# Second-layer biases of a mixture of experts: one spread load per expert and one addition per block, or one gathered row per token

## The chip, the cores and the metric

The kernel runs on one core of a Trainium2 chip. The metric is the device time of one execution in microseconds (us), a median over runs. The profile is one further execution, recorded by the hardware profiler. TensorE (PE) does matmuls, VectorE (DVE) and ScalarE (ACT) work on tiles, GpSimd (POOL) issues transfers whose rows are picked by an index, and SyncE (SP) issues the large loads. Each engine works through its own list of instructions in the order in which it was built.

## The reference, cut to what matters

625 tokens of width 768 pass a two-layer graph attention network, and then a transformer block whose second half is a mixture of 8 experts with one expert per token. With one expert per token the weight of the choice is a softmax over one value, so it is 1.

```python
x = x + _L0_gnn_ref(_layernorm(x), edge_index, ...)          # two graph attention layers
x = x + _L0_ffn_ref(_layernorm(x)[None], ...)[0]
# inside _L0_ffn_ref:
x = x + out @ Wp + bp                                         # after causal attention, 12 heads
h2 = _ln(x, ln2_g, ln2_b).reshape(-1, d)
w, sel = jax.lax.top_k(h2 @ Wg, 1)                            # the expert of each token
hid = jax.nn.relu(jnp.einsum('nd,edf->enf', h2, W1) + b1[:, None, :])
y = jnp.einsum('enf,efd->end', hid, W2) + b2[:, None, :]      # b2: one row of 768 per expert
return x + moe                                                # moe: row n of y[sel[n]]
```

The bias in question is `b2`: every token gets the row of its own expert added once.

## The kernel before, in words

Tokens are held in T = 5 tiles of R = 125 rows. The stages follow each other on one core: the graph layers (up to about 340 us), attention, routing (mixed into the end of attention, about 540 to 607 us), and the experts (from 577 us to the end).

**Two things per token go through DRAM to be sorted by expert.** `xg` receives the normalised rows `h2`, from which an expert computes; `xr` receives the rows `xid` (the sum to which the expert's output is added, plus the token's number in a last column). Both are written by scatters: an indirect DMA issued by POOL with the row numbers `pos[t]`. `send(t)` computes `pos[t]` and scatters tile t of `h2`; `send_sums(t)` adds `xx` (the attention block's own sum) to `x` on DVE and scatters the tile of `xid`.

**Tile by tile.** `project(t, i, ...)` makes the attention output for one half of a tile and adds it to `xx` (with `bn_stats` of the norm behind it), `second_norm(t)` makes `h2`, `gate_turn(t)` and `gate(t)` make the logits, `choose(t)` takes the best expert into `ef` and its one-hot row into `oh`. The PE, DVE and ACT order of this part is written by hand as far as the block that ends with `whole_norm(4)`; within it, an instruction from later in the source can still be placed between by the scheduler if nothing holds it.

**The first expert starts early.** After three tiles (TA = 3) the expert that is most frequent in tile 0, `first_e`, is known. Its first up to 128 rows are loaded: `xa` from `xg` (POOL, L1269) and `ra` from `xr` (POOL, L1279). `turn_rows` transposes `xa` on PE, and a DVE and an ACT copy bring the result to `xaT` (L1088). PE cannot start `first_step` before `xaT` is there. During `first_step` the last two tiles are routed, and a chain of small DVE instructions makes the table of blocks.

**Then a loop over blocks**: each block has up to 128 + 32 rows of one expert. Its rows come from `xg` (`rows_in`) and from `xr` (into `rw`, and `rq` for the narrow rest). `Wide.into` and `Wide.out_of` are the two layers; `narrow` does the same for 32 rows. `load_first` and `load_second` load the next expert's weights (18.9 MB in 12 transfers) through SP as PE releases the buffers; where the next block has the same expert, the transfers are skipped by a condition. The first expert's weights are loaded in pieces named `ew0_0`, `ew1_0` (in their own pool) and then `ew0_1`, `ew1_1`, `ew0_2`, `ew1_2`, whose memory was attention's and the routing's before; so these wait until its last reader is done.

**The second bias** is a tile `b2b` of [128, 768]: `load_bias(e)` loads the row of expert e into all 128 partitions through SP (384 KB), once for the first expert, once before the loop and at the end of each turn of the loop, the latter two under the condition that the expert changes. `prepare(rows, idx, M)` adds it to the block's rows on DVE, ahead of `add_up`, which adds the PE results from PSUM, and of `scatter_out`, which writes the rows to the output.

Of the kernel before, what the change touches and what calls it, by code (L numbers as in the profile page):

```python
# [9 lines left out]
F32 = mybir.dt.float32  # L10
F16 = mybir.dt.float16
BF16 = mybir.dt.bfloat16
I32 = mybir.dt.int32
# [8 lines left out]
R = 125  # L22
T = N // R
XR = 120
D = 768
# [18 lines left out]
B = 128  # L44
# [4 lines left out]
Q = 32  # L49
U = B // Q + 1  # L50
TA = 3
RE = 640
# [17 lines left out]
def gnn_moe_kernel(ctx: ExitStack, tc: tile.TileContext, p, out):  # L70
    nc = tc.nc
# [10 lines left out]
    xr = dram.tile([NR, D + 1], F32, name="xr")  # L82
# [3 lines left out]
    x = xid[:, :, :D]  # L86
# [68 lines left out]
    with tc.tile_pool(name="gnn", bufs=1) as gp:  # L155
# [4 lines left out]
        rows = gp.tile([R, HEADS, N], F32, tag="rows", name="rows1")  # L160
        al = gp.tile([R, 2, T, HEADS], F32, tag="al", name="al1")

        def load_bc(tag, v, n, eng=nc.gpsimd):
            b = gp.tile([B, D if tag == "bc4" else HC], F32, tag=tag, name=tag)
            eng.dma_start(b[:, :n], row_bcast(v, n))
            return b[:R, :n]
# [465 lines left out]
        with tc.tile_pool(name="gw", bufs=2, reuse_waits="tile") as gw, \  # L632
# [158 lines left out]
            b2 = load_bc("bc2", p["L0_gnn_b2"], D)  # L791
# [70 lines left out]
    ap = rt.enter_context(tc.tile_pool(name="rt", bufs=1, side="right", reuse_waits="tile"))  # L862
    with tc.tile_pool(name="att", bufs=1, reuse_waits="tile") as a1, \
# [32 lines left out]
        xx = ap.tile([R, T, D], F32, name="xx")  # L896
# [31 lines left out]
        ra = sx.tile([B, D + 1], F32, tag="ra", name="ra")  # L928
# [209 lines left out]


        ef = ap.tile([R, T], F32, name="ef")  # L1140
        oh = ap.tile([R, T, E], BF16, name="oh")
        io8 = ap.tile([R, E], F32, name="io8")
        nc.gpsimd.iota(io8, pattern=[[1, E]], base=0, channel_multiplier=0,
# [3 lines left out]
        def best(a):  # L1147
            mx = small.tile([R, 8], F32, name="mx")
            nc.vector.max(mx, a)
            mi = small.tile([R, 8], U32, name="mi")  # L1150
            nc.vector.max_index(mi, mx, a)
            return mi[:, 0:1]

        def choose(t):
            nc.vector.tensor_copy(ef[:, t:t + 1], best(lg[:, t, :]))
            nc.vector.tensor_scalar(oh[:, t, :], io8, ef[:, t:t + 1], None, op0=OP.is_equal)

        def choose_first():

            pc = ps.tile([128, 512], F32, tag="tp", name="pc")  # L1160
            nc.tensor.matmul(pc[:R, :E], ones, oh[:, 0, :], start=True, stop=True)
            c0 = small.tile([R, E], F32, name="c0")
            nc.vector.tensor_copy(c0, pc[:R, :E])
            nc.vector.tensor_copy(origin, best(c0))
            nc.vector.tensor_copy(first, origin[0:1, :])
# [3 lines left out]
        def scatter(buf, src, t):  # L1169
            s = nc.gpsimd.indirect_dma_start(  # L1170
                out=buf, out_offset=bass.IndirectOffsetOnAxis(ap=pos[t], axis=0),
                in_=src, in_offset=None)
            for q in scatters.setdefault(id(buf), []):
                tc.declare_no_dep(s.ins, q.ins, reason="other rows")
            scatters[id(buf)].append(s)

        def send(t):

            pk = ps.tile([128, 512], F32, tag="tp", name="pk")
            for s in range(t + 1):  # L1180
                nc.tensor.matmul(pk[:R, :E], before if s == t else ones, oh[:, s, :],
                                 start=(s == 0), stop=(s == t))
            rank = small.tile([R, E], F32, name="rank")
            slot = small.tile([R, 1], F32, name="slot")
            nc.vector.tensor_tensor_reduce(rank, pk[:R, :E], oh[:, t, :], scale=1.0, scalar=0.0,
                                           op0=OP.mult, op1=OP.add, accum_out=slot)
            nc.vector.tensor_scalar_add(slot, slot, float(Q))
            nc.vector.scalar_tensor_tensor(pos[t], ef[:, t:t + 1], float(RE), slot, op0=OP.mult,
                                           op1=OP.add)
            scatter(xg, h2[:, t, :], t)  # L1190

        def send_sums(t):
            nc.vector.tensor_add(x[:, t, :], x[:, t, :], xx[:, t, :])
            scatter(xr, xid[:, t, :], t)
# [73 lines left out]
        first_e = nc.values_load(first[0:1, 0:1], engines=[SP, pool], min_val=0, max_val=E - 1)  # L1268
# [6 lines left out]
        mix(last, (latest,), "tp")  # L1275
        gate_turn(3)
        for t in range(TA):
            send_sums(t)
        nc.gpsimd.dma_start(ra, xr[ds(first_e * RE + Q, B), :])  # L1279
        project(4, 1, most)  # L1280
        gate(3)
        for i in range(2):
# [6 lines left out]
        pe_order.close()  # L1289

    early.close()
    W1, W2, b2 = p["L0_ffn_W1"], p["L0_ffn_W2"], p["L0_ffn_b2"]
    w1, w2 = [None] * NFC, [None] * NFC

    def piece(ew, l, c):
# [13 lines left out]
            return [nc.sync.dma_start(to[i], of_e[i], **cond) for i in range(2)]  # L1309
        return [load_half(w1[c][:, k:k + 3, :], e, c, k, **cond) for k in range(0, KD, 3)]  # L1310

    def load_bias(e, **cond):
        nc.sync.dma_start(b2b, b2[ds(e, 1), :].to_broadcast([B, D]), **cond)

    ewa = ctx.enter_context(tc.tile_pool(name="ewa", bufs=1, reuse_waits="tile"))
    mw = ctx.enter_context(tc.tile_pool(name="mw", bufs=2, reuse_waits="tile"))
    sp = ctx.enter_context(tc.tile_pool(name="sps", bufs=2, space=PSUM, reuse_waits="tile"))
# [3 lines left out]
    piece(ewa, 1, 0)  # L1321
    load_piece(first_e, 0, 0)
    load_piece(first_e, 1, 0)
    b2b = mw.tile([B, D], F32, name="b2b", bufs=1)
    load_bias(first_e)

    hb = [mw.tile([128, 512], F32, name=f"hb{i}", bufs=1) for i in range(2)]
    hT = [mw.tile([128, 4, 128], F32, name=f"hT{c}", bufs=1) for c in range(2 * NFC)]
# [92 lines left out]
    def prepare(rows, idx, M):  # L1421

        nc.vector.tensor_copy(idx[:M], rows.bitcast(I32)[:M, D:D + 1])
        nc.vector.tensor_add(rows[:M, :D], rows[:M, :D], b2b[:M])

    def add_up(rows, py, M):

# [51 lines left out]
    with tc.issue_after(begun.ins):  # L1479
        for t in range(TA, T - 1):  # L1480
            send(t)
            send_sums(t)
        gate_turn(T - 1)
        gate(T - 1)
    with tc.issue_after(next(step_a).ins):
        send(T - 1)
        send_sums(T - 1)


    pc = ps.tile([128, 512], F32, tag="p1", name="cnt")  # L1490
# [121 lines left out]
    def behind(s, first):  # L1612
        tc.add_manual_dep(s.ins, first.ins.name, ORDER)
# [5 lines left out]
    def unit(w, b):  # L1619

        return (w if b == 0 else (w + 2) >> 2 if b < 3 else w >> 2) & 1

    def rows_in(row, w=None):

        rows = xg[ds(row, U * Q), :].rearrange("(b r) (q c) -> b q r c", r=Q, q=4)
        for b in range(U):
            cond = {} if w is None else dict(cond=unit(w, b))
            nc.gpsimd.dma_start(xb[:, b, :], rows[b], **cond)
# [5 lines left out]

    row_0 = nc.values_load(table[0:1, 1, 0:1], engines=[pool], min_val=0, max_val=NR - U * Q)
    rows_in(row_0)
    first_made, = step_a
    right.close()
    routing.close()
# [48 lines left out]
    word_0 = word(0, SP)  # L1688
    load_first((word_0 >> 8) & 7, (word_0 >> 7) & 1)
    load_second((word_0 >> 8) & 7, (word_0 >> 7) & 1)  # L1690
    load_bias((word_0 >> 8) & 7, cond=(word_0 >> 7) & 1)

    n_blk = nc.values_load(nblk[0:1, 0:1], min_val=1, max_val=NS)
    sp_order.close()
    with tc.For_i(0, n_blk, 1, iteration_sync="reg_based") as i:
        w = word(i)
        then = (w >> 4) & 7, (w >> 3) & 1
        row, row_next = (nc.values_load(table[0:1, 1, ds(k, 1)], engines=[pool], min_val=0,
                                        max_val=NR - U * Q) for k in (i, i + 1))

        nc.gpsimd.dma_start(rq[:Q], xr[ds(row, Q), :], cond=unit(w, 0))
        for b in (1, 3):
            s = nc.gpsimd.dma_start(rw[(b - 1) * Q:(b + 1) * Q], xr[ds(row + b * Q, 2 * Q), :],
                                    cond=unit(w, b))
            behind(s, loads[b - 1])
        rows_in(row_next, word(i + 1, pool))
        bT, s = biases((w >> 8) & 7)
        behind(s, first_load)
        of = {M: Wide(M, xT[:, :, Q:Q + M], bT) for M in (64, B)}

        with tc.If((w & 2) == 2) as c64:
            with tc.manual_schedule(engines={PE}):
                of[64].begin()
        with c64.Else():
            with tc.If((w & 4) == 4):
                with tc.manual_schedule(engines={PE}):
                    of[B].begin()
        with tc.If((w & 1) == 1) as c32:
            narrow(bT, *then)
        with c32.Else():  # L1720
            nc.vector.memset(iq, N)
            load_first(*then)
        turn_next()

        def scatter_narrow(*others):
            s = scatter_out(rq, iq, Q)
            for o in others:
                tc.declare_no_dep(s.ins, o.ins, reason="other rows")
            behind(s, first_load)

        def finish(M):
            prepare(rw, iw, M)
            with tc.manual_schedule(engines={PE}):
                of[M].end()
            load_second(*then)
            add_up(rw, pw, M)
            s = scatter_out(rw, iw, M)
            behind(s, first_made)
            scatter_narrow(s)

        with tc.If((w & 2) == 2) as d64:
            finish(64)
        with d64.Else():
            with tc.If((w & 4) == 4) as d128:
                finish(B)
            with d128.Else():
                behind(nc.gpsimd.dma_start(idle, xr[0:1, :8]), loads[4])
                load_second(*then)
                scatter_narrow()
        load_bias(then[0], cond=then[1])  # L1750


# [29 lines left out]
```

## Time and profile before

| | us |
|---|---|
| median of 3 runs | 983.27 (983.01 to 986.92) |
| the profiled execution's own time | 985.54 |
| its span in the profile | 983.2 |
| PE busy in the span | 948.3 (96%) |
| DVE busy | 449.3 (46%) |
| ACT busy | 295.8 (30%) |
| POOL busy | 65.7 (7%) |

An instruction line of the timeline has: start, duration, engine, source line, operation, output <- inputs, how many instructions were merged, and in brackets how long the engine was idle before and what released it. PEld is PE's loading of stationary operands, which overlaps PE. SPq is SP's list of DMA issues. The landing time of a transfer goes from the start of its issue to the arrival of its last byte.

### The profile page before, as it was taken

The page shows a single profiled execution, that of the slowest core. Times are in us where ns is not written, and L with a number is a line of the kernel's source. Part 1 is how long each engine was busy: PE and PEld are TensorE (multiplying, and loading weights), DVE is VectorE, ACT ScalarE, POOL GpSimd, SP SyncE. Part 2 cuts the span into 40 slices and gives each one's busy share as a digit, 9 for nine tenths or more (in the row PEclk, how much of TensorE's full clock was granted, in tenths as well). Part 3 has the DMA queues.
Part 4 walks back from the last instruction along what each step waited for, and adds up shares of the span by engine and source line. Part 5 has one row for each costly group of instructions (what it writes and reads, how often), then busy time and mean ns, then how long its engine had stood idle before and what let it go on. Part 6 is the DMA issues. An engine that isn't in the chain of part 4 may idle for free. (4 is left out here: it accounts for less than half of the span.)

```text
span 983.2 us, 15216 instructions
## 1 busy us (share of the span) xinstructions
PE 948.3 (96%) x4675; PEld 586.7 (60%) x4676; DVE 449.3 (46%) x1310; ACT 295.8 (30%) x776; POOL 65.7 (7%) x147
## 2 busy tenths in 40 slices
PE   8999999999999999999999989999999999989995
PEld 5555665777555556677775645546454656544653
DVE  8978892783384920475555654112111213121303
ACT  6897550562230110444442302101100121101302
POOL 2000000000000100000000113010100110210000
PEclk9999999999999999999999999999999999999998
DMA  9404103001500356999300599410789999999993
GB/s 273 176 1 172 34 1 144 1 1 49 112 1 0 94 149 115 416 406 382 126 1 1 215 341 332 109 43 8 261 292 335 367 363 409 342 403 369 407 404 144
DMA packets 87727, 191.69 MB, mean 195 GB/s; under 512 B 34405, under 2 KB 36317, under 8 KB 87674
## 3 DMA queue, kind: packets, MB, share of 16 engines
q1 hardware_dynamic: 80441, 175.22, 50.1%
q0 software_dynamic: 7152, 15.64, 5.1%
q8 instruction: 29, 0.48, 0.2%
q14 instruction: 25, 0.20, 0.1%
q10 hardware_dynamic: 80, 0.16, 0.1%
HBM read 213.29 MB, written 39.55 MB: 257 GB/s over the span
## 5 line engine op out<-in xcount | busy, mean ns | idle before, releaser
L1398 PE MATMUL pw<-ew,hT 128*64 128x384 f32 (+1 forms) x672 | 159.8, 487 | 6.4 <-DMA ew<-in_L_ffn_W_dram 1.9
L1398 PEld LDWEIGHTS pw<-ew,hT 128*64 128x64 f32 (+1 forms) x672 | 101.4, 160 | 59.1 <-issue 15.0
L1372 PE MATMUL ph<-ew,xid 128*64 128x512 f32 (+1 forms) x432 | 127.7, 594 | 3.4 <-DMA ew<-in_L_ffn_W_dram 1.8
L1388 ACT ACTIVATE hT<-tph,bT 128x64 f32<-128x64 f32 (+1 forms) x168 | 40.8, 361 | 268.4 <-PE tph L1383 173.6
L1372 PEld LDWEIGHTS ph<-ew,xid 128*64 128x64 f32 (+1 forms) x432 | 53.6, 155 | 66.8 <-issue 59.8
L692 PE MATMUL agg<-xl,zT 125*125 125x256 f32 (+1 forms) x300 | 79.9, 417 | 2.9 <-ACT zT L681 2.9
L1375 DVE COPY hb<-ph 128x512 f32<-128x512 f32 x28 | 19.4, 691 | 135.4 <-PE ph L1372 135.4
L692 PEld LDWEIGHTS agg<-xl,zT 125*125 125x125 f32 x300 | 54.5, 188 | 21.4 <-ACT zT L681 4.4
L410 PE MATMUL pp<-w,yT 128*125 128x512 f32 x120 | 53.5, 595 | 0.2 <-DMA xid<-in_x_dram 0.2
L800 PE MATMUL ph<-wr,h1T 128*125 128x384 f32 x160 | 52.6, 486 | 0.0
L1435 DVE TENSOR_TENSOR rw<-rw,pw 64x192 f32<-64x192 f32 (+1 forms) x48 | 12.9, 315 | 86.7 <-PE pw L1398 86.4
L759 PE MATMUL ph<-w,h1T 128*125 128x384 f32 x160 | 52.4, 486 | 0.0
L256 ACT ACTIVATE step<-halved,past 125x210 f16<-125x210 f16 x138 | 50.9, 461 | 0.0
L1030 DVE CUSTOM_DVE_ANT_0 e<-sc,later 125x625 f32<-125x625 f32 (+4 forms) x60 | 29.8, 542 | 36.2 <-PE sc L1007 36.2
L174 PE MATMUL ph<-wr,yT 128*125 128x512 f32 x96 | 42.2, 594 | 1.0 <-ACT pr L419 0.8
L1034 ACT ACTIVATE e<-e,of 125x625 f32<-125x625 f32 (+4 forms) x60 | 35.7, 596 | 23.3 <-DVE of L1030 23.3
L759 PEld LDWEIGHTS ph<-w,h1T 128*125 128x125 f32 x160 | 30.0, 187 | 21.2 <-issue 0.5
L800 PEld LDWEIGHTS ph<-wr,h1T 128*125 128x125 f32 x160 | 29.8, 187 | 21.1
L1098 PE MATMUL po<-wpj,aT 128*125 128x384 f32 x120 | 41.7, 492 | 0.4 <-DVE xx L1102 0.4
L941 PE MATMUL pv<-L_ffn_Wv,hT 128*125 128x384 f32 x120 | 39.5, 486 | 0.0
L978 PE MATMUL pq<-hT,L_ffn_Wq 128*128 128x313 f32 (+1 forms) x144 | 39.4, 429 | 0.0
L978 PE MATMUL pq<-hT,L_ffn_Wk 128*128 128x313 f32 (+1 forms) x144 | 39.4, 429 | 0.0
(336 smaller groups left out, 1262.1 us busy)
## 6 DMA issues: line engine op xcount, KB each, us to landing
ew<-in_L_ffn_W_dram SPq DMA_DIRECT2D x108, 1536.0 KB
xr<-zt SPq DMA_DIRECT2D x5, 3076.0 KB
xg<-zt SPq DMA_DIRECT2D x5, 3072.0 KB
w<-in_L_gnn_W_dram SPq DMA_DIRECT2D x4, 1536.0 KB
wr<-in_L_gnn_Wr_dram SPq DMA_DIRECT2D x4, 1536.0 KB
xid<-xg POOLq DMA_DIRECT2D x40, 96.0 KB, 10.3
b2b<-in_L_ffn_b_dram SPq DMA_DIRECT2D x9, 384.0 KB
rw<-xr POOLq DMA_DIRECT2D x14, 192.2 KB
```

Source lines behind the costliest of these rows:

```text
L174: nc.tensor.matmul(pp[:R, :], yT[:, c, cols(t)], part(wr1, KD, c, i, 512), start=(c == 0), stop=(c == KD - 1))
L256: nc.scalar.activation(o, halved[:, :n], AF.Sign, bias=at, scale=-1.0)
L410: nc.tensor.matmul(pp[:R, :], yT[:, c, cols(t)], part(w1, KD, c, i, 512), start=(c == 0), stop=(c == KD - 1))
L692: nc.tensor.matmul(self.agg[:R, c0:c0 + n], zT[:, s, :], xl[:, s, x0:x0 + n], start=(s == 0), stop=(s == T - 1))
L759: nc.tensor.matmul(ph[:R, :384], h1T[:, c, cols(t)], part(w2, KH, c, i, 384), start=(c == 0), stop=(c == KH - 1))
L800: nc.tensor.matmul(ph[:R, :384], h1T[:, k, cols(t)], part(wr2, KH, k, i, 384), start=(k == 0), stop=(k == KH - 1))
L941: nc.tensor.matmul(pp[:R, :384], hT[:, c, cols(t)], w[i][:, c, :], start=(c == 0), stop=(c == KD - 1))
L978: nc.tensor.matmul(pp[:, :b - a], w[:, c, c0:c0 + 128], hT[:, c, a:b], start=(c == 0), stop=(c == KD - 1))
L1098: nc.tensor.matmul(po[t, i][:R, :384], aT[:, c, cols(t)], wpj[i][:, c, :], start=(c == 0), stop=(c == KD - 1))
L1372: mm = nc.tensor.matmul(ph[g * M:(g + 1) * M, :C].rearrange("p (j f) -> p j f", f=128), self.xT[:, k, :], w[:, k, g], start=(k == 0), stop ...
L1388: self.made = nc.scalar.activation(hT[c][:, k, r], tp[:, k, r], AF.Relu, bias=self.bT[:, f:f + 1])
L1398: mm = nc.tensor.matmul(pw[i][g * M:(g + 1) * M, :384], hT[c][:, k, g * M:(g + 1) * M], w[:, self.block(c, g, k), i * 384:(i + 1) * 384], ...
```

## The change

The bias row is added per token before the rows are sorted. `choose(t)` keeps the expert's number as an integer `ei` as well (a POOL copy). After `add_sums(t)` has added `xx` into `x`, that tile of `xx` is not needed any more, and an indirect DMA from POOL gathers row `b2[ei]` for each of its 125 tokens into it. `send_sums(t)` then adds `xx` a second time and scatters. The tile `b2b`, its loads and the addition in `prepare` are gone. The load of `ra` moves from ahead of `project(4, 1, ...)` to behind the first `rows_in`.

```diff
+        ei = ap.tile([R, T], I32, name="ei")
...
         def choose(t):
             nc.vector.tensor_copy(ef[:, t:t + 1], best(lg[:, t, :]))
             nc.vector.tensor_scalar(oh[:, t, :], io8, ef[:, t:t + 1], None, op0=OP.is_equal)
+            nc.gpsimd.tensor_copy(ei[:, t:t + 1], ef[:, t:t + 1])
...
+        def add_sums(t):
+            nc.vector.tensor_add(x[:, t, :], x[:, t, :], xx[:, t, :])
+            nc.gpsimd.indirect_dma_start(
+                out=xx[:, t, :], out_offset=None, in_=p["L0_ffn_b2"],
+                in_offset=bass.IndirectOffsetOnAxis(ap=ei[:, t:t + 1], axis=0))
 
         def send_sums(t):
             nc.vector.tensor_add(x[:, t, :], x[:, t, :], xx[:, t, :])
             scatter(xr, xid[:, t, :], t)
...
         for t in range(TA):
-            send_sums(t)
-        nc.gpsimd.dma_start(ra, xr[ds(first_e * RE + Q, B), :])
+            add_sums(t)
         project(4, 1, most)
...
-    def load_bias(e, **cond):
-        nc.sync.dma_start(b2b, b2[ds(e, 1), :].to_broadcast([B, D]), **cond)
...
-    b2b = mw.tile([B, D], F32, name="b2b", bufs=1)
-    load_bias(first_e)
...
     def prepare(rows, idx, M):
 
         nc.vector.tensor_copy(idx[:M], rows.bitcast(I32)[:M, D:D + 1])
-        nc.vector.tensor_add(rows[:M, :D], rows[:M, :D], b2b[:M])
...
     with tc.issue_after(begun.ins):
         for t in range(TA, T - 1):
             send(t)
+            add_sums(t)
+        for t in range(TA):
             send_sums(t)
         gate_turn(T - 1)
         gate(T - 1)
     with tc.issue_after(next(step_a).ins):
         send(T - 1)
-        send_sums(T - 1)
+        add_sums(T - 1)
+        for t in range(TA, T):
+            send_sums(t)
...
     rows_in(row_0)
+    nc.gpsimd.dma_start(ra, xr[ds(first_e * RE + Q, B), :])
...
-    load_bias((word_0 >> 8) & 7, cond=(word_0 >> 7) & 1)
...
-        load_bias(then[0], cond=then[1])
```

Places in the source and places in an engine's list differ here, since the scheduler is free to move `send_sums`' additions forward. In the built programs the order on PE and on ACT is the same as before. On DVE the second additions of tiles 0, 1 and 2 stand between `gate(3)`'s instructions and the `xaT` copy, that of tile 3 ahead of the last step of tile 4's norm, and that of tile 4 at the beginning of the small instructions that make the table. On POOL the three gathers of tiles 0 to 2 stand directly behind the load of `xa`, where the three scatters to `xr` stood.

More of the change, by code (lines that the diff above doesn't have):

```diff
@@ L1291, in gnn_moe_kernel @@
     early.close()
-    W1, W2, b2 = p["L0_ffn_W1"], p["L0_ffn_W2"], p["L0_ffn_b2"]
+    W1, W2 = p["L0_ffn_W1"], p["L0_ffn_W2"]
     w1, w2 = [None] * NFC, [None] * NFC
```

## The prediction

> **What bounds the kernel now.** First the page's table of engines, then who PE waits for. The columns are: total us, times, longest.
>
> ```profile
> PE 948.3 (96%) x4675; PEld 586.7 (60%) x4676; DVE 449.3 (46%) x1310; ACT 295.8 (30%) x776; POOL 65.7 (7%) x147
> ...
> PE pw L1398 <- DMA ew<-in_L_ffn_W_dram: 1.9, 1, 1.9
> PE ph L1372 <- DMA ew<-in_L_ffn_W_dram: 1.8, 2, 1.0
> PE ph L1372 <- SPq L1695: 1.6, 1, 1.6
> PE pq L1672 <- DMA ew<-in_L_ffn_W_dram: 1.5, 1, 1.5
> ```
>
> PE is the bound: some 35 us of the span without it. Whatever stops PE counts in full, and a gain exists only where PE waits: 5.2 us for expert weights, 1.6 us for SP at the loop's entry. Next the timelines of PE, DVE and POOL around the routing, since the change puts its gathers there.
>
> ```profile
> 575.42 1.05 PE L1086 MATMUL tpx<-ident,xa 128*128 128x128 f32 x6 [1.29 <-DMA xa<-xg]
> 577.55 12.07 PE L1372 MATMUL ph<-ew,xaT 128*128 128x512 f32 x24 [1.08 <-DVE xaT L1088]
> ...
> 598.71 10.57 PE L1372 MATMUL ph<-ew,xaT 128*128 128x512 f32 x24
> ```
>
> ```profile
> 572.77 0.17 DVE L1136 COPY lg<-pl 125x8 f32<-125x8 f32 x1 [2.47 <-PE pl L1134]
> ...
> 574.36 0.56 DVE L1105 BATCH_NORM_STATS2 st<-xx 125x6 f32<-125x384 f32 x1
> ...
> 575.89 0.94 DVE L1193 TENSOR_TENSOR xid<-xid,xx 125x768 f32<-125x768 f32 x1
> ...
> 576.86 0.64 DVE L1088 COPY xaT<-tpx 128x512 f32<-128x512 f32 x1
> ```
>
> ```profile
> 571.96 0.61 POOL L1269 DMA_DIRECT2D xa<-xg  x1 [9.45 <-DMA xg<-h,pos]
> 573.08 1.21 POOL L1170 DMA_INDIRECT xr<-xid,pos  x1 [0.51 <-DMA b2b<-in_L_ffn_b_dram]
> 574.60 1.19 POOL L1170 DMA_INDIRECT xr<-xid,pos  x1 [0.30 <-DVE bT L1336]
> 576.10 1.79 POOL L1170 DMA_INDIRECT xr<-xid,pos  x1 [0.30 <-DVE st L1105]
> 590.26 0.61 POOL L1279 DMA_DIRECT2D ra<-xr  x1 [12.37 <-DMA xr<-xid,pos]
> ```
>
> PE has run out of attention work at 574.1 us and waits for DVE's `xaT`. DVE is just in time: everything from 572.77 to 576.86 stands ahead of `xaT`. POOL gets no index transfer out between 562.5 and 573.1, because `xa` waits for the scatters. Last, how long transfers take to land (min/median/max; the scatters at L1170, then `xa`, then an output scatter while DMA is otherwise quiet), and SP's bias loads.
>
> ```profile
> DMA to landing us min/median/max: 8.6/10.5/13.9
> ```
>
> ```profile
> DMA to landing us min/median/max: 3.3/3.3/3.3
> ```
>
> ```profile
> out_dram<-ra,iw POOLq DMA_INDIRECT x1, 3.3
> ```
>
> ```profile
> 751.38 0.35 SPq L1313 DMA_DIRECT2D b2b<-in_L_ffn_b_dram  x1
> ...
> 795.31 6.58 SPq L1313 DMA_DIRECT2D b2b<-in_L_ffn_b_dram  x1
> ...
> 848.56 5.12 SPq L1313 DMA_DIRECT2D b2b<-in_L_ffn_b_dram  x1
> ```
>
> **Removed.** (1) Ten additions of 0.94 to 0.97 us in `prepare`, 9.5 us of DVE. All lie beside matmuls: the one in `first_step` ends at 634.3 and the next DVE work waits for PE until 644.6; the last (969.97 to 970.92) is followed by additions whose last input leaves PE at 973.0. Worth nothing. (2) The bias loads. Six are executed, 567.41, the three above, 905 and 957; 393 kB at the 406 GB/s of the 900 to 950 window are 0.97 us of DMA each. DMA is full from about 723 to 965, and PE's weight waits lie at 814, 868, 873 and 876. Three executed loads (751, 795, 849) are queued ahead of the last of them: 2.9 us come back. Bounds: 0, if PE's releases and not DMA time these loads, and 5.2, all the waits. (3) The loop's entry: SP spends 647.3 to 647.9 on a skipped bias load before L1695, for which PE waits 1.6 us. I take 0.6 (0 to 1.6). The load at 567.41 competed with the third `xg` scatter; without it `xa` could come up to 1 us earlier. I count nothing.
>
> **Added and moved.** POOL's five copies of `ei` ([125, 1]) have no row. Tile 0 to 2's have 1.8 us or more between `ef` and `pos`, for which the scatter behind them waits anyway: hidden, up to 1.8 us each; a slower one would push the gathers back by the excess. Five gathers at a scatter's issue price (1.2 us) fit in POOL's idle time. Five more DVE additions of 0.94 us: what matters is what they wait for. In the built DVE order the additions marked + are new:
>
> ```
> lg<-pl (gate 3)
> + xid<-xid,xx  waits for the gather of tile 0
> Max, MaxIndex
> + xid<-xid,xx  waits for the gather of tile 1
> ef, oh, xx<-xx,po
> + xid<-xid,xx  waits for the gather of tile 2
> BNStats, xx<-xx,po, BNStats, xid<-xid,xx (tile 4)
> xaT<-tpx
> ```
>
> So `xaT`, and with it PE, now waits for three gathers which POOL can issue only behind `xa`: at 573.08, 574.60 and 576.10, where the three `xr` scatters stood. If the third lands at L, `xaT` starts at L + 0.94 (the addition) + 2.50 (574.36 to 576.86, all still to be done). PE's stall is L + 3.44 - 576.86.
>
> How long does a gather take? None is in the trace. The floor is 3.3 us, `xa` (the same bytes by a direct load, before the weights queue up) or the quiet output scatter; `ra<-xr`, a direct load under partial load, took 6.2; the five scatters to `xg` and five to `xr` took 8.6 to 13.9. The nearest are the three `xr` scatters that stood in this very place: the same 125 rows, the same queue, beside the same 6.3 MB of weights (`ew0_1`, `ew1_1`) which SP issues from 574.26. The two of them that begin before 575 have a median of 11.0, and the third, on which `ra` waits until 590, has the 13.9. Their mean is 12.0, which I take since reading DRAM replaces writing it: L = 588.1, stall = 14.7 us. With 3.3 the stall is 6.0, with 6.2 it is 8.9, with 13.9 it is 16.6.
>
> The Trainium skill's page "DMA: Bandwidth & Descriptors" (section on the anatomy of one SWDGE DMA) gives a transfer issued by GpSimd about 2.0 us plus bytes over 436 GB/s. By that rule, as an estimate, 384 kB land in 2.9 us and the time would be 985.4; it fits the quiet row of 3.3, and the rows under load are three to four times that.
>
> The stall's restart at a low clock is already paid in the trace: the 24 matmuls at 577.55 take 12.07 us against 10.57 later, with a granted clock of 0.50 from 578 to 580. I add nothing. The page "TensorE: Matmul & The Clock Gate" (Part 1) says that the array runs at half rate until about 3.4 us of work have passed after an idle window; that would cost an estimated 1.7 us per restart, 0.2 more than the 1.5 already there.
>
> What is late next? Behind the stalled additions on DVE stands tile 4's norm, used by PE 14 us later (590.68). On POOL, `xr`'s first scatter waits for the first addition, and behind it stand tile 3's `ei` and gather. That gather is issued near 589 and its addition stands ahead of the copies `hb`, which PE needs at 589.67 + 14.7 = 604.4: hidden if it lands within 13 us. Tile 4's gather is issued near 610.8 and holds the table, `rows_in` and the moved `ra`. At 610 DMA is idle, so at 3.3 to 10.5 us it lands by 621; the table takes 8 us, `rows_in` and `ra` some 15 more, needed at 646 to 659 (631.5 and 644.6 plus the stall): hidden. SP's `ew0_2` and `ew1_2` may now wait for these additions since they take over `xx`'s memory; `ew0_2` is needed at 614.72 + 14.7 = 629.4 and takes 7.8 us: hidden up to an issue at 621.6. After that all is paced by PE and moves with it.
>
> **Sum.** 14.7 - 2.9 - 0.6 = +11.2 us. On the profiled execution's own 985.54 that is 996.7; that execution lies 2.3 above the median of 983.27, so I forecast 994.5.
>
> **Rivals.** *Short landing, not slower.* If gathers land like `xa`, in 3.3 us, the sum is 6.0 - 3.5 = +2.5: 985.8, and with the full 5.2 + 1.6 of the gains 982.5. For it: rows go to SBUF, the eight source rows are only 24 KB. Against: at 574.26 the weights enter and stay until about 590. It decides at +4.9 us, that is at a stall of 8.4, a landing of 5.7 us. *Slow landing and late weights.* If all gathers need 13.9 us the stall is 16.6; tile 4's gather, issued at 612.7, lands at 626.6, its addition ends at 627.5, `ew0_2` follows with two halves of 3.9 us to 635.3, and PE wants the second at 634.0: 1.3 more, +14.4: 997.7. For it: the third scatter. Against: DMA is quiet at 612. *The order is changed but the gathers are not waited for*: excluded, the additions read what the gathers write.
>
> **Numbers.** A measurement here can tell about 0.5% (4.9 us) from no change: 978.4 to 988.2. The forecast's case (landings from 5.7 us to about 13) has 0.58, slow landing 0.16, short landing 0.26, of which 0.04 for a time below 978.4, which none of my terms reaches. Slower 0.74, same 0.22, faster 0.04. Range 985.0 to 1000.0: it takes in the short landing's 985.8 and 997.7 with some 2 us on top, since no gather has a row.
>
> **What would show it.** Right: DVE idle before the new additions from about 573 on with the gathers named, PE idle before the `ph` line for 12 to 18 us, PE's weight waits down from 5.2 to about 2.3, everything after shifted alike. Wrong: `xaT` before 582, a second stall behind the table or `ew0_2`, or weight waits unchanged.

## The result, and the profile after

| | before | after |
|---|---|---|
| median, us | 983.86 (983.01 to 986.92, 4 runs) | 1002.19 (1000.63 to 1004.85, 4 runs) |
| the profiled execution's own time | 985.54 | 1000.63 |
| its span | 983.2 | 999.1 |

The change costs 1.8%: the ratio is 1.018, with a 95% interval of 1.0163 to 1.0198. By the medians that is 18.3 us, by the profiled executions 15.1 (spans: 15.9). The forecast was 994.5, +11.2 on the profiled execution, with a range up to 1000.0: the direction holds, the size does not.

The page of the changed kernel, its line of engines, then who PE waits for (total us, times, longest):

```profile
PE 946.9 (95%) x4675; PEld 584.1 (58%) x4676; DVE 444.8 (45%) x1305; ACT 296.0 (30%) x776; POOL 71.9 (7%) x157
```

```profile
PE ph L1374 <- DVE xaT L1088: 19.3, 1, 19.3
PE pw L1400 <- PEq L1723: 3.4, 3, 2.0
...
PE ph L1374 <- SPq L1700: 1.0, 1, 1.0
...
PE pw L1400 <- DMA ew<-in_L_ffn_W_dram: 0.8, 1, 0.8
PE ph L1374 <- DMA ew<-in_L_ffn_W_dram: 0.8, 1, 0.8
```

PE works as much as before; one wait of 19.3 us for `xaT` (1.1 before) is new. The waits for weights went from 5.2 to 1.6, the one for SP from 1.6 to 1.0. The timelines of DVE, POOL and PE at the same place as before:

```profile
582.37 0.96 DVE L1201 TENSOR_TENSOR xid<-xid,xx 125x768 f32<-125x768 f32 x1 [9.45 <-DMA xx<-in_L_ffn_b_dram,ei]
...
588.15 0.96 DVE L1201 TENSOR_TENSOR xid<-xid,xx 125x768 f32<-125x768 f32 x1 [4.47 <-DMA xx<-in_L_ffn_b_dram,ei]
...
591.55 0.96 DVE L1201 TENSOR_TENSOR xid<-xid,xx 125x768 f32<-125x768 f32 x1 [1.65 <-DMA xx<-in_L_ffn_b_dram,ei]
...
594.92 0.64 DVE L1088 COPY xaT<-tpx 128x512 f32<-128x512 f32 x1
```

```profile
573.00 1.25 POOL L1196 DMA_INDIRECT xx<-in_L_ffn_b_dram,ei  x1 [0.52 <-DVE lg L1136]
574.56 1.21 POOL L1196 DMA_INDIRECT xx<-in_L_ffn_b_dram,ei  x1 [0.30 <-issue]
576.08 1.21 POOL L1196 DMA_INDIRECT xx<-in_L_ffn_b_dram,ei  x1 [0.30 <-issue]
```

```profile
595.62 12.40 PE L1374 MATMUL ph<-ew,xaT 128*128 128x512 f32 x24 [19.26 <-DVE xaT L1088]
...
617.11 10.57 PE L1374 MATMUL ph<-ew,xaT 128*128 128x512 f32 x24
```

Three times DVE sits idle until a gather has landed: 9.4, 13.6 and 15.5 us after its issue (582.37 - 573.00, 588.15 - 574.56, 591.55 - 576.08). Behind the third come the 3.4 us of work that stood there already, then `xaT`, 18.1 us later than before (594.92 against 576.86).

Between four points of PE's timeline, the difference of the two spans comes apart (us):

| | before | after | difference |
|---|---|---|---|
| start to the first `ph` | 577.55 | 595.62 | +18.07 |
| first `ph` to the loop's first `ph` | 71.22 | 70.91 | -0.31 |
| the loop, to the end of the last `pq` | 324.21 | 320.10 | -4.11 |
| from there to the end of the span | 10.17 | 12.44 | +2.27 |
| span | 983.15 | 999.06 | +15.91 |

So the stall is 18.1, the removal of the bias loads wins 4.4, and 2.3 are lost at the very end, where no term of the prediction is.

What DMA does from 573 to 592 (views of the DMA queues before, then after: packets, MB, share of 16 engines; q1 is SP's queue with the weights, q0 POOL's with the rows):

```profile
q1 hardware_dynamic: 1446, 5.08, 70.9%
q0 software_dynamic: 752, 1.55, 25.7%
```

```profile
q1 hardware_dynamic: 878, 3.39, 63.0%
q0 software_dynamic: 885, 1.76, 32.7%
```

The engines are as full as before but move less: a weight packet takes 0.709 x 16 x 19 us / 1446 = 149 ns on average before and 218 ns after. (For packets of 4096 bytes between 578 and 590 the trace has a median of 159 and 231 ns.) POOL's queue gets 1.55 and 1.76 MB in these 19 us, 82 and 93 GB/s.

### The profile page after: what moved, and what is told of

Read it like the earlier page. It is cut to its first block, busy times and chain, and to the rows that moved or that the text cites. A ratio compares the mean times of both kernels' runs of the same rounds, so it can differ in the third digit from the quotient of the medians.

```text
span 999.1 us, 15157 instructions
## 1 busy us (share of the span) xinstructions
PE 946.9 (95%) x4675; PEld 584.1 (58%) x4676; DVE 444.8 (45%) x1305; ACT 296.0 (30%) x776; POOL 71.9 (7%) x157
## 5 line engine op out<-in xcount | busy, mean ns | idle before, releaser
L1374 PE MATMUL ph<-ew,xaT 128*128 128x512 f32 x72 | 33.6, 623 | 19.3 <-DVE xaT L1088 19.3
```

What stands on the lines that cost most here:

```text
L1374: mm = nc.tensor.matmul(ph[g * M:(g + 1) * M, :C].rearrange("p (j f) -> p j f", f=128), self.xT[:, k, :], w[:, k, g], start=(k == 0), stop ...
```

## The experiments

The theory: the loss is a wait that DVE's order creates, its length is the landing of the third gather, and the rest is small. The rivals: the gathers or their traffic cost by themselves, or a new wait behind the first takes its place. In the diffs `+` is against the changed kernel unless it says otherwise.

### The order on DVE

**e1_hold** queues the second additions behind PE's first work:

```diff
+        with tc.issue_after(copied_1.ins):        # the second copy to hb
+            for t in range(TA):
+                send_sums(t)
...
+    with tc.issue_after(v.tensor_copy(table, tabf[:, 2:, :]).ins):
+        for t in range(TA, T):
+            sent = send_sums(t)
```

> The changed kernel, but the second additions of tiles 0 to 2 (and with them the xr scatters) are queued on DVE only behind the second hb copy of the first expert's step, those of tiles 3 and 4 behind the copy that makes the table, and rows_in behind the last xr scatter. The gathers are issued where they were. Theory (the loss is the place of three additions ahead of xaT in DVE's list): PE's wait before the first ph line goes from 19.3 us back to about 1 us although the gathers still land 9 to 16 us after issue, and the gains at the tail stay (weight waits 1.6 instead of 5.2 us, about 0.6 at the loop's entry): about 983.9 - 3.6 to 5.2, that is 978.5 to 980.5 us. Rival 1 (the gathers' traffic itself delays the weights of the first expert): ph starts at 577 to 578, but PE waits for ew0_1 at about 590 for 2 to 5 us, total 981 to 985. Rival 2 (a second wait, for the later xr scatters, the table or ew0_2, takes the place of the first): a new PE wait of over 5 us between 600 and 660, total 985 or more.

Measured: 987.37 us, ratio 1.0033 (1.0015 to 1.005). In the waits of its PE:

```profile
PE ph L1375 <- DMA ew<-in_L_ffn_W_dram: 2.1, 2, 1.3
...
PE ph L1375 <- DVE xaT L1088: 1.2, 1, 1.2
```

The stall is gone (1.2 us), with the same gathers at the same place. So the order is the cause of the stall. But the time is not below the kernel before, and the wait for weights has a new item, between 617.8 and 619.1, for `ew0_2`. (The profiled execution, 984.6, is the lowest of the eight.) A second profile of this order is that of **e8_hold_tail** (e1_hold with the small load of e7_tail, below, on SP):

> The run e1_hold (the changed kernel with the second additions queued behind PE's first expert) with the same load of 8 values at the end of each turn. e1_hold had 987.4 us, a span of 982.8 in its profile, and 4.6 us at the end. If the end is mended by the load: 985 us by the median, no difference from the kernel before. If the end does not change: 987.4. A second profile also shows whether the first expert's late weights (1.3 us of PE's wait at 618) are larger in another execution: up to 6 us would explain why the other runs of e1_hold lie up to 7.5 us above its profiled one.

Measured: 988.32 us, ratio 1.0044 (1.0028 to 1.006). PE's timeline there:

```profile
616.65 2.81 PE L1375 MATMUL ph<-ew,xaT 128*128 128x512 f32 x6 [2.46 <-DMA ew<-in_L_ffn_W_dram]
620.90 2.84 PE L1375 MATMUL ph<-ew,xaT 128*128 128x512 f32 x6 [1.44 <-DMA ew<-in_L_ffn_W_dram]
```

In this execution the late weights cost 3.9 us. So rival 1 of e1_hold holds in kind: between 584 and 596 DMA moves 254 to 277 GB/s in e1_hold (407 to 416 before, from 584 to 590). But the piece that is late is `ew0_2` near 618, not `ew0_1` near 590, and the time is above the 981 to 985 that the rival gave. The end was not mended by the load (13.0 us after the last `pq`).

### What a gather takes

**e2_rows** reads 625 different rows, to see whether reading 8 rows over and over is slow:

```diff
-                out=xx[:, t, :], out_offset=None, in_=p["L0_ffn_b2"],
-                in_offset=bass.IndirectOffsetOnAxis(ap=ei[:, t:t + 1], axis=0))
+                out=xx[:, t, :], out_offset=None, in_=p["x"],
+                in_offset=bass.IndirectOffsetOnAxis(ap=xid.bitcast(I32)[:, t, D:D + 1], axis=0))
```

> The changed kernel, but the gathers read the token's own row of the input x (625 different rows) in place of one of the 8 rows of b2, so the output carries a wrong bias; everything else, the number of rows and bytes too, is the same. If reading the same 8 rows over and over is what is slow: the three gathers land 8 to 12 us after issue (as the xr scatters did in this place: 8.6 to 13.9), DMA moves about 400 GB/s from 578 to 590 in place of 275 to 307, and ph starts at about 590 to 592. If any gather of 125 rows beside the weights is that slow: landings 11.5 to 15.5 us, DMA 270 to 310 GB/s, ph at about 595.6, and the total stays at about 1000 us.

Measured: 1012.49 us, ratio 1.0281 (1.026 to 1.0302). The first four second additions on DVE:

```profile
581.18 0.96 DVE L1201 TENSOR_TENSOR xid<-xid,xx 125x768 f32<-125x768 f32 x1 [10.55 <-DMA xx<-in_x_dram,xid]
...
589.03 0.96 DVE L1201 TENSOR_TENSOR xid<-xid,xx 125x768 f32<-125x768 f32 x1 [6.81 <-DMA xx<-in_x_dram,xid]
...
592.42 0.96 DVE L1201 TENSOR_TENSOR xid<-xid,xx 125x768 f32<-125x768 f32 x1 [2.09 <-DMA xx<-in_x_dram,xid]
...
595.61 0.96 DVE L1201 TENSOR_TENSOR xid<-xid,xx 125x768 f32<-125x768 f32 x1 [1.43 <-DMA xx<-in_x_dram,xid]
```

The repeated rows are not it: with issues at 573.18, 574.74, 576.24 and 577.75 the landings are 8.0, 14.3, 16.2 and 17.9 us. Tile 3's row numbers are known early here, so that four gathers, not three, stand ahead of `xaT`; the last two additions come 3.4 and 3.2 us after the one before, and the first `ph` starts 4.1 us later than in the changed kernel (599.67). Another 5.6 us are lost between there and the loop, 3.9 of them in a wait of PE for `hb`, and 2.2 in the loop.

**e3_quiet** keeps the weights out while the gathers run:

```diff
+        if c == 1:
+            tc.add_manual_dep(loads[-2].ins, second[TA - 1].ins.name, ORDER)
```

> The changed kernel, but the load of ew0_1 and all that SP issues behind it wait for the second addition of tile 2, so that the three gathers land without weight transfers beside them; DVE's order is unchanged. If the landing time is contention with the weights: the gathers land 3.3 to 6 us after issue, the third at 580 to 582, ph starts at 583 to 586 (stall 6 to 9 us); the weights then start some 8 us later, and PE may wait for ew0_1 about 598 for up to 5 us. If the gathers are slow by themselves (125 descriptors to 8 rows): landings of 11 us or more, ph at 592 or later, and the late weights come on top.

Measured: 995.19 us, ratio 1.0105 (1.0085 to 1.0126).

```profile
580.59 0.96 DVE L1203 TENSOR_TENSOR xid<-xid,xx 125x768 f32<-125x768 f32 x1 [6.18 <-DMA xx<-in_L_ffn_b_dram,ei]
...
582.84 0.96 DVE L1203 TENSOR_TENSOR xid<-xid,xx 125x768 f32<-125x768 f32 x1 [0.94 <-DMA xx<-in_L_ffn_b_dram,ei]
```

Issued at 574.38, 575.94 and 577.45, the gathers land after 6.2, 6.9 and 7.1 us, and PE's wait is 10.9 instead of 19.3. So the weights beside them are over half of the third's landing time (7.1 of 15.5), a third of the first's (6.2 of 9.4). 6 to 7 us is what three gathers need without weights, twice the 3.3 of `xa`; no run has a single gather on quiet queues. The late weights cost PE next to nothing here (71.6 us from the first `ph` to the loop, 70.9 in the changed kernel).

**e5_direct** replaces each gather by a direct load of the same size:

```diff
+            nc.gpsimd.dma_start(xx[:, t, :], p["x"][t * R:(t + 1) * R, :])
```

> The changed kernel, but each gather is replaced by a direct load of 125 rows of the input x into the same tile, from the same queue in the same place (so the output carries a wrong bias): the bytes, the rows and the waits stay, only the row index goes. Beside the gathers a weight packet of 4096 bytes takes 231 ns in the changed kernel, 159 ns beside the scatters of the kernel before, and the gathers land in 9.4 to 15.5 us. If the indexed form is what is slow: weight packets near 160 ns, DMA near 400 GB/s from 580 to 590, landings of 3.3 to 7 us as the direct loads xa and ra had, ph at 583 to 588, total 986 to 992 us. If it is rows being written into SBUF beside the weights, indexed or not: weight packets at 220 ns or more, 270 to 310 GB/s, landings of 11 to 16 us, ph at 592 to 596, total 997 to 1002 us.

Measured: 994.62 us, ratio 1.0099 (1.0079 to 1.012). Windows of DMA (the last two columns are DMA's busy share and GB/s):

```profile
582.00:584.00 2.00, 0.00 (x0) 0.00 (x0) 1.30 (x5) 0.00 (x0) 0.63 (x2) 0.50 1.00 267
584.00:586.00 2.00, 0.00 (x0) 0.00 (x0) 1.29 (x3) 0.00 (x0) 1.23 (x1) 0.50 1.01 369
586.00:588.00 2.00, 0.00 (x0) 0.00 (x0) 1.97 (x5) 0.00 (x0) 1.18 (x1) 0.50 1.05 410
```

Neither expectation as a whole. Loads of 125 rows into `xx` slow the weights beside them without any index: a weight packet of 4096 bytes takes 220 ns (median, 578 to 586), DMA moves 249 to 267 GB/s until the last of four loads has landed at 585, and 410 after that. What it is in these loads stays open. In the kernel before, `ra`, a direct load of 128 rows into SBUF, leaves weight packets of 3072 bytes at 122 to 124 ns (594.0 to 595.5), while beside tile 3's gather in e13_hold_quiet, below, they take 187 to 195 ns (604 to 606). So it is not any row load into SBUF. The direct loads are sooner there than the gathers: issued in 0.55 us each from 572.42 on, they have a longer start on the weights at 574, and land in 5.0 to 11.1 us, four of them in less time than three gathers.

**e6_one** leaves only tile 2's gather of the three ahead of `xaT`:

```diff
+            if t not in (0, 1):
                 nc.gpsimd.indirect_dma_start(
```

> The changed kernel without the gathers of tiles 0 and 1 (their bias rows are left out of the output, and xx is added a second time in their place); tile 2's gather and its place ahead of xaT stay, and it now stands first in POOL's queue behind xa, issued at about 573. In the changed kernel the three gathers moved about 70 GB/s beside the weights, 1.15 MB in 16 us, and landed one after the other, 9.4, 13.6 and 15.5 us after issue. If they wait for one another in the queue's share of DMA: tile 2's gather lands 8 to 10 us after issue, like tile 0's in the changed kernel; ph starts at 585 to 587 (stall 8 to 9.5 us), total 990 to 993 us. If each gather needs 12 us or more beside the weights whatever stands ahead of it (the way the prediction summed it): ph at 588.5 to 593 and 994 to 999 us.

Measured: 990.92 us, ratio 1.0064 (1.0045 to 1.0082). One line of DVE and one of PE:

```profile
580.51 0.96 DVE L1202 TENSOR_TENSOR xid<-xid,xx 125x768 f32<-125x768 f32 x1 [5.81 <-DMA xx<-in_L_ffn_b_dram,ei]
```

```profile
584.57 13.63 PE L1375 MATMUL ph<-ew,xaT 128*128 128x512 f32 x24 [8.20 <-DVE xaT L1088]
```

Issued at 573.08 and first in the queue, the same gather lands after 7.4 us instead of 15.5, with the same weights beside it. So its place in the queue decides: POOL's queue gets a share, and the last of three lands when the bytes of all three have gone through. In that place it also starts earlier, 1.5 us ahead of the weights, where the third gather of the changed kernel is issued 1.8 us behind them; how much of the 8 us that start is worth was not separated. (Tile 3's gather in e6_one, issued at 577.77 behind two scatters, takes 14.9 us.) The Trainium skill's page "DMA: Bandwidth & Descriptors" (section "Queues, rings and completion order") says that a DMA engine takes turns between the queues that have work for it, a packet at a time. The measured share, 93 of 271 GB/s for POOL's queue beside the weights, fits that; the turns themselves are in no trace.

### What the removal is worth

Against the kernel before: **e9_adds** takes out the loads and keeps the additions, **e10_loads** the reverse, **e4_nobias** takes out both.

```diff
-    load_bias((word_0 >> 8) & 7, cond=(word_0 >> 7) & 1)     # e9_adds, e4_nobias
-        load_bias(then[0], cond=then[1])                     # e9_adds, e4_nobias
-        nc.vector.tensor_add(rows[:M, :D], rows[:M, :D], b2b[:M])   # e10_loads, e4_nobias
```

> The kernel before without the second biases altogether (the tile b2b, its loads and its additions are left out, nothing is gathered, so the output lacks b2). It measures the removal alone. If PE's weight waits at the end are set by how much DMA has to bring: they go from 5.2 us to 1.6 to 2.3, with 0.6 at the loop's entry: -3.5 to -5.2, that is 978.5 to 980.5 us. If they are set by PE's releases: weight waits unchanged and 982.5 to 984 us. If DVE's additions were worth anything, more than 5.2 us would come back.

> The kernel before without the bias loads before and in the loop (the first expert's row stays in b2b, so the others get a wrong bias); the ten additions on DVE stay. If the gain of the removal is the loads alone: as e4_nobias, weight waits 1.6 to 2.3 us in place of 5.2, 982 to 983 us. If the additions had a share in it: 983 us or more, nearer to the kernel before. The end of the program after the last output transfer: 4.0 to 4.6 us if it hangs on the loads that are gone, 2.2 if on the additions.

> The kernel before without the ten additions of the bias (so b2 is left out of the output), all its loads kept. If the additions are hidden beside PE's matmuls, as the prediction has them: the time of the kernel before within 0.1%, weight waits 5.2 us, 2.2 us at the end. If they are not: up to 9.5 us less.

Measured: e4_nobias 982.34, ratio 0.9973 (0.9962 to 0.9984); e9_adds 981.80, 0.9972 (0.996 to 0.9984); e10_loads 985.48, 1.001 (0.9999 to 1.002). The waits of PE in e9_adds, then in e10_loads:

```profile
PE pw L1398 <- DMA ew<-in_L_ffn_W_dram: 0.8, 1, 0.8
...
PE ph L1372 <- DMA ew<-in_L_ffn_W_dram: 0.8, 1, 0.8
PE pq L1672 <- DMA ew<-in_L_ffn_W_dram: 0.5, 1, 0.5
```

```profile
PE ph L1372 <- DMA ew<-in_L_ffn_W_dram: 1.8, 2, 1.0
...
PE pw L1398 <- DMA ew<-in_L_ffn_W_dram: 1.6, 1, 1.6
...
PE pq L1671 <- DMA ew<-in_L_ffn_W_dram: 1.1, 1, 1.1
```

The additions are worth nothing and the loads 2.8 us, as a net of 4 to 6 won up to the last `pq` and 1.8 to 2.5 lost at the end (below). In e4_nobias the waits for weights fell to 1.7 us, as in the first branch of its expectation, but the time is above the 978.5 to 980.5 given with it, by what the end lost. No run has the loads out and the end kept short without the gathers.

Can the loads be had cheaper? **e7_tail** puts a load of 8 values into e4_nobias where the bias load stood, **e11_act** and **e11_pool** let ACT or POOL issue the kernel before's bias load in the loop.

```diff
+        nc.sync.dma_start(last, b2[ds(then[0], 1), :8], cond=then[1])    # e7_tail
...
+        load_bias(then[0], nc.scalar, cond=then[1])                      # e11_act; nc.gpsimd in e11_pool
```

> The kernel before without the second biases (b2 is left out of the output), as in the run e4_nobias, but with one load of 8 values under the same condition at the end of each turn of the loop, where the bias load stood. All four kernels without that load need 4.0 to 4.6 us from the end of the last output transfer to the end of the span, the kernel before 2.2. If the end depends on what stands last in SP's part of the loop: 2.2 us again, and a span some 2 us under the 980.8 of e4_nobias, 980 to 981 us by the median. If it does not: 4.0 us or more and the 982.3 us of e4_nobias.

> The kernel before, with the bias load at the end of each turn issued by ACT instead of SP; bytes, condition and everything else stay. e9_adds, without the loads, won 2.8 us, but e7_tail, with a load of 8 values in SP's place, won nothing by its median. If what the bias load costs is its place in SP's list (the next turn's weights are issued behind it): 982 to 983 us, as without the loads. If it costs by its bytes on the DMA engines: no difference from the kernel before (about 985), weight waits about 5.2 us.

> The same with POOL as the issuer. If SP's place is what costs: 982 to 983 us. If the bytes: about 985. Against a gain even then: POOL issues the loads of the next block's rows in this loop, and a bias load ahead of them could make these late, 986 or more.

Measured: e7_tail 984.69, ratio 0.9999 (0.999 to 1.0007); e11_act 987.95, 1.0027 (1.0014 to 1.0039); e11_pool 989.34, 1.0046 (1.0032 to 1.0059). Moving the load off SP is a loss, and both have the longer end (12.5 and 14.1 us). Why 8 values per turn cost as much as a full row by the median stays open: the profiled execution of e7_tail, the lowest of its 12, has the loop of the kernels without the load (321.1 us).

### The end of the program

The trace shows what the 2.3 us are. While POOL drains its last output transfer for 5.1 us, SP works through a list of closing waits, and once in it SP pauses for 2.4 us. In all 17 traces an 8 KB packet of an instruction queue lies inside that pause. What is different is how many of SP's executed instructions are still behind the pause:

| kernel | ahead of the pause | behind the pause | last `pq` to the end, us |
|---|---|---|---|
| before | 1135 | 21 | 10.2 |
| e10_loads | 1135 | 20 | 10.2 |
| e11_act | 1087 | 13 | 12.5 |
| e7_tail | 1129 | 8 | 12.5 |
| e9_adds | 1087 | 5 | 12.6 |
| after | 1087 | 3 | 12.4 |

The pause stands at the same place of the list in every kernel: the loop runs seven turns, and where a load in it makes a turn of SP 8 instructions longer (7 in e7_tail), its six repetitions are the 48 (42) more ahead of the pause. So what is missing in the changed kernel, 18 instructions of the list, is missing behind the pause, and the pause comes out from under POOL's drain. Of SP's waits at the end, in the kernel before and then in the changed one, only the latter have it, as SP waiting for itself:

```profile
SPq L1778 <- PEq L1778: 1.2, 3, 0.5
```

```profile
SPq L1782 <- PEq L1782: 3.3, 2, 3.2
SPq L1782 <- SPq L1782: 2.4, 1, 2.4
```

**e12_pad** makes the list longer, with no other change:

```diff
+    with tc.issue_after(load_piece(first_e, 1, 0)[-1].ins):
+        for _ in range(6):
+            nc.values_load(first[0:1, 0:1], engines=[SP], min_val=0, max_val=E - 1)
```

> The changed kernel with six more reads of the same value into SP's registers (18 instructions) at a point where SP has nothing to do, between the loads of ew1_0 and ew0_1. If the 2.3 us at the end come from where a pause of 2.4 us falls in SP's list: in the changed kernel it has 3 instructions of SP behind it, in the kernel before 21; with 18 more it stands some 21 from the end, before POOL's last drain is done, and from PE's last matmul to the end it is about 10.2 us: 2 to 2.4 us less, 999.8 to 1000.2 by the median. If the end has another cause: 12.4 us and 1002.2.

Measured: 1002.32 us, ratio 1.018 (1.0164 to 1.0195). In the trace the pause has 21 instructions behind it again, and from the last `pq` to the end it is 10.7 us instead of 12.4: the cause is shown, for 1.7 of the 2.3 us. In the time it does not appear. In the profiled execution the first `ph` comes 0.5 us later, the first expert takes 0.5 longer and the loop 2.5. The most in the loop is PE's wait in the first turn and what follows (e12_pad, then the changed kernel):

```profile
686.19 7.10 PE L1402 MATMUL pw<-ew,hT 128*64 128x384 f32 x32 [2.26 <-PEq L1725]
```

```profile
684.91 5.48 PE L1400 MATMUL pw<-ew,hT 128*64 128x384 f32 x32 [1.98 <-PEq L1723]
```

The window behind it in e12_pad (the granted clock, PE's clock as a share of full speed, is the third number from the end):

```profile
686.00:690.00 4.00, 3.81 (x14) 2.38 (x16) 1.64 (x2) 0.00 (x0) 0.94 (x1) 0.57 0.02 4
```

After 2.26 us of idling the granted clock is 0.57 here, and the same 32 matmuls take 7.10 us instead of 5.48; after 1.98 us, in the changed kernel, it stays at 1. A wait that is 0.3 us longer, whose reason is not known, and 1.6 us of slow matmuls are 1.9 of the loop's 2.5; 0.4 of the rest is a later wait for weights.

### Both remedies together

**e13_hold_quiet** holds the additions back only behind tile 4's norm and keeps the weights away until they are done; **e14_hold_quiet_pad** adds the longer list.

```diff
+        with tc.issue_after(normed_by[T - 1].ins):     # the last step of whole_norm(4)
+            for t in range(TA):
+                send_sums(t)
...
+        if c == 1:
+            tc.add_manual_dep(loads[-2].ins, second[TA - 1].ins.name, ORDER)
```

> The changed kernel with the second additions of tiles 0 to 2 queued on DVE directly behind tile 4's norm, which is behind xaT (those of tiles 3 and 4 behind the table as in e1_hold), and with the loads of ew0_1 and all that SP issues behind it waiting for the third of these additions. If contention between the gathers and the weights was what e1_hold still paid (weight packets of 240 in place of 160 ns, ew0_2 1.3 to 3.9 us late): ph starts at 577 to 578, the gathers land within 7 us, by 585, no wait for ew0_2, 982 to 985 us. If the weights cannot start 10 us later without being late: waits for ew0_1 near 598 or ew0_2 near 615 of 3 us or more, 986 us or more.

> The run e13_hold_quiet with the 18 more instructions of e12_pad on SP. If the pause is the cause of the longer end: 2 to 2.4 us less than e13_hold_quiet, that is 980 to 983 us, a version faster than the kernel before by some 2 to 4 us. If not: the time of e13_hold_quiet.

Measured: 992.91, ratio 1.0077 (1.0059 to 1.0095), and 991.83, 1.008 (1.0062 to 1.0098). PE in e13_hold_quiet:

```profile
577.97 13.62 PE L1379 MATMUL ph<-ew,xaT 128*128 128x512 f32 x24 [1.15 <-DVE xaT L1088]
...
623.63 5.25 PE L1379 MATMUL ph<-ew,xaT 128*128 128x512 f32 x6 [4.16 <-DMA ew<-in_L_ffn_W_dram]
```

The stall is gone and the gathers land within 8 us, but without the stall the weights have no time to spare: `ew0_1` is issued at 585.65, 11 us later than in the changed kernel, and behind it `ew0_2` is 4.2 us late. That is the second half of the expectation. The list made the end shorter again (10.9 against 12.6), and again the medians hardly show it. No version that beats the kernel before came out of this.

## Why the prediction was right or wrong

**The stall's cause: right.** DVE idles from 573 on with the gathers named, `xaT` and PE wait behind it, and e1_hold takes the wait away by queueing the additions later on DVE, with the gathers where they were. The work behind the third addition is 3.37 us from its start to `xaT` (591.55 to 594.92), 3.44 in the sum.

**The stall's size: the step that failed.** It is "Their mean is 12.0, which I take": the third gather landed after 15.5, so the stall is 18.1 and not 14.7. The mean was the wrong use of the right rows. The three transfers stand in one queue and the last lands last (after 9.4, 13.6 and 15.5 us; the scatters after 8.6, 13.4 and 13.9), and the same gather in first place took 7.4 (e6_one). So the row for the third was the third scatter's 13.9, a stall of 16.6. Beyond that the third gather landed 1.6 us later than that scatter (the first 0.8, the second 0.2). It fits that the packets beside gathers are slower than beside scatters (231 and 159 ns; e5_direct 220 ns without an index), so the reason "since reading DRAM replaces writing it" pointed the wrong way; but no run isolates these 1.6 us. The rival of slow landing, 13.9 for all, was nearest; its late `ew0_2` did not come, since that was issued at 604.6, well ahead of the 621.6 it could bear.

**The short landing: refuted.** 3.3 us was `xa` alone; three gathers without weights need 6.2 to 7.1 (e3_quiet). The estimate of 2.9 us from the formula of the Trainium skill's page "DMA: Bandwidth & Descriptors" (section on the anatomy of one SWDGE DMA) is not met by a gather in any run; none has one gather alone on quiet queues.

**The removal: right in kind.** DVE's additions are worth nothing (e10_loads, 1.001). Without the loads more came back than the 2.9 and 0.6 of the sum: waits for weights 5.2 to 1.6, the loop 4.1 us shorter, and 0.65 at the loop's entry, of which the slower start of the first `ph` (12.40 against 12.07 us) took 0.3 back. That start cost 1.8 against the later 10.57, where the prediction reckoned with the 1.5 already there.

**The end: not in the sum.** SP's list lost 18 instructions, and a pause of 2.4 us came out from under POOL's drain: +2.3. e12_pad takes 1.7 of it back.

**Hidden work: right.** Tile 3's gather landed after 11.5 us, within the 13 it had; the table, `ra` and `ew0_2` made no second stall, and PE's points shift alike, +17.8 at the loop's start and +18.3 up to 768, until the weight waits that are gone bring it to +13.6 at the last `pq`.

So in the profiled executions: 18.1 for 14.7, -4.4 for -3.5, +2.3 for nothing. By their own times these two executions are 15.1 apart; the other 3.2 us of the medians' difference are the spread of single executions, since the profiled one of before lies 1.7 above its median and that of after 1.6 below. One more fall of the clock as in e12_pad fits the 1.6, and the other three executions of the changed kernel have a mean granted clock of 0.985 beside the profiled one's 0.986; but they have no trace.

**The base: chance.** The forecast took off 2.3 us because the profiled execution lies above a median of three. In 80 further executions of the kernel before, in the rounds of the experiments, the median is 985.2, so that 985.54 was a usual one and the step made the forecast too low by about as much. Against 985.2 the change costs some 17 us, if the rounds compare.

## What to carry to other kernels

A transfer placed for free on an idle queue is paid by whoever stands behind its reader: look up in the built order what an engine has queued behind the instruction that will wait, and hold that instruction back if a critical copy is among it. Of several transfers in one queue beside a full one, price the last by the bytes of all at the queue's share, and look for the row in the same position, not for a mean. Then ask what the held-back transfer does to the bulk traffic: in e1_hold and e13_hold_quiet the gain of taking the wait away went to late weights.

## What the runs showed of the hardware

- Loads of 125 rows into `xx`, indexed or direct, slow the weight packets beside them from 159 to 220 to 231 ns (medians for 4096 bytes), and all of DMA from 364 to 416 GB/s down to 250 to 310, while its engines show no idle time. Scatters of the same rows out of SBUF do not, and `ra`, a direct load of 128 rows, did not either (3072 bytes: 122 to 124 ns). What makes the difference was not isolated.
- PE's granted clock fell to a half for some 3.4 us after waits of 2.11, 2.19, 2.26, 2.27, 2.33 and 2.54 us, and not after 1.98, 2.00, 2.06, 2.21 and 2.46. Where the same matmuls can be compared, a fall costs 1.6 to 1.7 us (in e12_pad 7.10 against 5.48). The Trainium skill's page "TensorE: Matmul & The Clock Gate" (Part 1) speaks of an idle window of about 3.4 us; here two thirds of that were enough in six cases. The page also says that its window runs free, which would fit the mixed results between 2.1 and 2.5; no run tests it. A wait that grew by 0.3 us has so cost 1.9.
- SP pauses 2.4 us (3.0 in one trace) at one place of its instruction list, with an 8 KB instruction packet inside. Whether that is seen depends on what runs beside it, so 18 instructions more or less on an engine that does nothing critical moved the end by 1.7 to 2.3 us.
